# The last block's feed-forward in tiles of 128 rows, its elementwise steps on VectorE and ScalarE

## The chip, the cores and the metric

The kernel runs on one core of a Trainium2 chip. The metric is the device time of one execution in microseconds; the time of a kernel is the median of its runs. An execution under the profiler also leaves a trace, whose span runs from the first to the last instruction that it shows.

## The reference

One transformer layer in float32: attention with 16 heads of 16, a residual and a layer norm, then a gated feed-forward whose three products work on inputs and weights rounded to a 4-bit floating-point grid in blocks of 16, a residual and a layer norm. There are 4 sequences of 2048 rows of 256; the hidden width is 704.

```
def fp4_quant_dequant(x):                  # blocks of 16 along the last dim
    scale = max(max(|xb|) / 6, 1e-12)
    q = _GRID[searchsorted(_MID, |xb / scale|)] * sign(xb) * scale

x = layernorm(x + softmax(q @ k.T / 4) @ v @ Wo.T)
gate = fp4_linear(x, w_gate);  y = fp4_linear(x, w_up)
x = layernorm(x + fp4_linear(silu(gate) * y, w_down))
```

## The kernel before

The work is cut into blocks of 512 rows (QB), four to a sequence, 16 in all, and each block into four groups of four heads: 64 steps. A step has 16 periods, one per 128 rows of keys (NKT). In each period TensorE computes the row maxima's products for a step further ahead (pm, reduced by VectorE into mx), the products of keys and queries (pe, exponentiated by ScalarE into e), and adds the values into av. This is written out period by period in the program's main loop, and TensorE keeps that order.

Everything else is cut into pieces, generators that yield an estimate of what they cost, and the function period takes one piece (two before the first step) between the attention's parts of each period, from the deque queue, or from urgent for what the next step waits for. The elementwise steps that belong to a piece are put off by a few periods with later, so that no engine is asked for them too early. One such chain is a block's feed-forward: once its four groups are done, normalize has written the block's attention output, transposed, as two tiles oT (128 x 512), and chain(b, qb) is put into the queue. While the following block's attention runs, the pieces of feed_forward lie between its parts. The last block has no attention after it: after the main loop, a second loop runs periods until all deques are empty.

feed_forward first loads the block's 512 rows of x as x1 (four tiles of 128 rows). residual multiplies oT by woT (py), ScalarE copies the bank out (read), GpSimd adds it to x1, VectorE takes the moments, and layer_norm's other steps are GpSimd's. Quantization (fp4) works on two tiles of 128 rows at once: VectorE takes the blocks' maxima, scales, reciprocals and the rounding terms m; GpSimd multiplies by the reciprocal (line 157), adds and subtracts m (163, 164) and multiplies by the scale (165). TensorE transposes the result (ptq), ScalarE copies it to xqT. gated makes, for each tile of 128 rows and each half of the hidden width (352 columns), the products pg and pu; ScalarE copies them out as g and u and takes tanh of half of pg as a; three steps make h = (a * g + g) * u (lines 537, 538, 551). In the last block these three, and the second fp4's own engine steps, run on VectorE for tiles 1 and 3 and on GpSimd for 0 and 2; elsewhere always on GpSimd. h is quantized, transposed by TensorE (pth), copied to hT by ScalarE (turned, two tiles together), and down multiplies it by wdT: for each half of the 256 output columns six products of 128 columns (pz), which ScalarE copies out and GpSimd adds to x1. out_rows normalizes two tiles and stores them.

PSUM has three banks of the pool ps_x and, once the attention is over, alternately those of ps_m. The tiles e rotate over ten buffers. TensorE's queue holds its instructions in the order in which the code issues them; for the other engines the language's own scheduler places them, and may weave two independent sequences. Each engine then runs its queue in order, and engines wait for each other by semaphores. The stores and loads here are all issued by SP.

Of the kernel before, what the change touches and what calls it, by code (L numbers as in the profile page):

```python
# [33 lines left out]
I32 = mybir.dt.int32  # L34
# [17 lines left out]
LN_EPS = 1e-5  # L52
LEAD = 20
LAG = 2
LEAST = 300.0
PSUM = bass.MemoryType.PSUM
DRAM = bass.MemoryType.DRAM
# [16 lines left out]
def block_kernel(  # L74
# [41 lines left out]
    def later(periods, step, rest=0):  # L116

        state = {"done": None}
        due.append((clock["now"] + periods, step, state))
        return lambda: state["done"] is not None and clock["now"] >= state["done"] + rest  # L120
# [21 lines left out]
        nc.scalar.copy(t, bank)  # L142
        return t

    def fp4(pool, t, tag, gain=1.0, engine=None):
# [8 lines left out]
        engine = engine or nc.gpsimd  # L154
        engine.tensor_scalar(rs, rs, gain * TIES_DOWN, 1.0, ALU.mult, ALU.mult)
        xn = pool.tile([p, nb, FB], F32, tag="xn" + tag, name="xn", bufs=3 if tag else 2)
        engine.tensor_tensor(xn, t, rs.unsqueeze(2).to_broadcast([p, nb, FB]), ALU.mult)

        def rounded():
            m = pool.tile([p, nb, FB], F32, tag="m" + tag, name="m", bufs=1)  # L160
            nc.vector.tensor_single_scalar(m.bitcast(I32), xn.bitcast(I32), EXPONENT, ALU.bitwise_and)
            nc.vector.tensor_scalar(m, m, 1.0, ROUND, ALU.max, ALU.mult)  # L162
            engine.tensor_tensor(xn, xn, m, ALU.add)  # L163
            engine.tensor_tensor(xn, xn, m, ALU.subtract)  # L164
            engine.tensor_tensor(xn, xn, sc.unsqueeze(2).to_broadcast([p, nb, FB]), ALU.mult)  # L165

        return xn, later(1, rounded, 4 if tag == "" else 2)


    ident = const.tile([P, P], F32, tag="ident", name="ident")  # L170
# [252 lines left out]
    def exponentials(s, kt, i):  # L423
        kb, col = kt // QT, kt % QT * P
        pe = [psum("pe") for _ in range(2)]
        for j in range(2):
            rows = slice(R * j, R * j + R)
            matmul(pe[j], k_sb[s, i, kb][rows, col : col + P], q_sb[s, i][rows, :], start=True, stop=True)
        for j in range(2):
            e = p1.tile([P, QB], F32, tag="e", name="e", bufs=10)  # L430
            nc.scalar.activation(e, pe[j], AF.Exp, scale=SCALE)  # L431
            e_sb[s, kt, 2 * i + j] = e

# [83 lines left out]
                later(3, lambda tiles=tiles: xq.append(fp4(p2, tiles, "")))  # L517
            yield 900

    def gated(xqT, h, t, engine):  # L520
        for half in range(2):
            cols = slice(half * FH, (half + 1) * FH)
            pg = psum("pg")
            for kc in range(KC):
                matmul(
                    pg[:, :FH],
                    xqT[:, kc, t * P : (t + 1) * P],
                    wgT[:, kc, cols],
                    start=(kc == 0),
                    stop=(kc == KC - 1),  # L530
                )

# [3 lines left out]
            nc.scalar.activation(a, pg[:, :FH], AF.Tanh, scale=0.5)  # L536
            engine.tensor_mul(a, a, g)  # L537
            engine.tensor_add(a, a, g)  # L538
# [12 lines left out]
            engine.tensor_mul(h[:, cols], a, u)  # L551
            yield 1200

    def turned(hq, tiles, hT):
# [29 lines left out]

    def feed_forward(b, qb, between):
        rows = slice(qb * QB, (qb + 1) * QB)
        last = b == B - 1 and qb == NQB - 1
# [12 lines left out]
        for kc in range(KC):  # L600
            pt = psum("ptq")
            for t in range(QT):
                q = xq[t // 2][0].rearrange("p (t b) f -> p t (b f)", t=2)
                transpose(pt[:, t * P : (t + 1) * P], q[:, t % 2, kc * P : (kc + 1) * P], ident)
            nc.scalar.copy(xqT[:, kc, :], pt)
            yield 500
        hq = {}

        def gate(t):

            engine = nc.vector if last and t % 2 else nc.gpsimd
            h = p2.tile([P, FF], F32, tag="h", name="h")
            yield from gated(xqT, h, t, engine)
            blocks = h.rearrange("p (b f) -> p b f", f=FB)
            later(1, lambda: hq.update({t: fp4(p2, blocks, "h", gain=0.5, engine=engine)}))
# [23 lines left out]
        out_rows(2)  # L639


    queue, urgent = deque(), deque()
# [57 lines left out]
    for n in range(-LEAD, N + LAG):  # L700
        m = n + LEAD
        (sm, im), (s, kt), (sv, kv) = divmod(m, NKT), divmod(n, NKT), divmod(n - LAG, NKT)
        if m in (8, 10, 12, 14):
            if m == 8:
                load_q(1)
            load_k(1, m // 2 - 4)
        if n == 0:
            load_v(0)
        if kt == 3 and 0 <= n and s + 1 < len(steps):
            load_v(s + 1)  # L710
        if n > 0 and kt % QT == 0:
            ahead, kb = divmod(n - QT + 2 * NKT, NKT)
            if ahead < len(steps):
                b, qb, g = steps[ahead]
                c = str(g * HG // NC)
                if kb == 0:
                    assert (b, qb, "q" + c) in projected
                    load_q(ahead)
                assert (b, kb // QT, "k" + c) in projected
                load_k(ahead, kb // QT)  # L720

        for i in range(NP):
            if m < N:
# [12 lines left out]
        period(1 if n >= 0 else 2)  # L736
    banks["more"] = True
    while urgent or queue or due:
        period(1)

# [3 lines left out]
_INS = [  # L744
    "L0_attn_x",
# [29 lines left out]
```

## Time and profile before

| | |
|---|---|
| runs | 3693.88, 3696.45, 3697.93 us |
| median | 3696.45 us |
| profiled execution | 3695.37 us, its span 3693.6 us |
| granted TensorE clock, mean of the span | 0.982 of full speed |
| TensorE matmul busy | 3540.7 us (96%) |
| VectorE busy | 2805.0 us (76%) |
| ScalarE busy | 2694.0 us (73%) |
| GpSimd busy | 1293.4 us (35%) |
| last oT written by ScalarE | at 3604.2 us |
| end of the last arithmetic instruction | at 3690.4 us |

In the profile, PE is TensorE's matmul, PEld its weight loads, DVE is VectorE, ACT ScalarE, POOL GpSimd, SP the engine that issues the DMAs. A row of a group or of the order of time gives the line of the kernel, the engine, the operation, the tiles written and read with their shapes, and the time of one in microseconds or, where said, nanoseconds; in brackets stands how long the engine was idle before, and who ended that. Matmuls and transposes carry the line of a helper, so they are told apart by their tiles. The chain of waits follows the work that ended last back from its end, at each step to what released it.

### The profile page before, as it was taken

The numbers are of one execution on the slowest core, as the hardware profiler recorded it, in microseconds if no ns is written. First come the engines' busy times: TensorE is split into PE (matmuls) and PEld (weight loads), VectorE is DVE, ScalarE is ACT, GpSimd is POOL, SyncE is SP. The second block draws the span as 40 slices with busy tenths as digits, with TensorE's granted clock in tenths as the row PEclk, the third lists the DMA queues.
The fourth block names the chain that finished last, engine by engine and source line by source line (L and its number), as shares of the span: only waits on it lengthen the run. The fifth ranks groups of instructions, "written<-read, shape, count | busy, mean of one in ns | idle before, by whom it ended". The sixth has DMA issues, their size and how long they took to land.

```text
span 3693.6 us, 57860 instructions
## 1 busy us (share of the span) xinstructions
PE 3540.7 (96%) x21396; PEld 1602.0 (43%) x21396; DVE 2805.0 (76%) x3250; ACT 2694.0 (73%) x5452; POOL 1293.4 (35%) x1542
## 2 busy tenths in 40 slices
PE   5889999999999999999999999999999999999995
PEld 4433444444444444444444444444443434444343
DVE  3777777787787877878787787778778788878834
ACT  2667777777777777777777777777777777777772
POOL 0331432424243242423424243342424325241425
PEclk8899999999999999999999999999999999999997
DMA  6643333223232332323323232322322221222100
GB/s 217 188 137 117 93 91 105 81 85 115 68 114 84 94 94 85 109 70 109 95 78 106 85 97 88 97 89 74 113 75 63 75 79 57 75 68 86 47 7 6
DMA packets 197954, 334.18 MB, mean 90 GB/s; under 512 B 26024, under 2 KB 75560, under 8 KB 197672
## 3 DMA queue, kind: packets, MB, share of 16 engines
q1 hardware_dynamic: 196280, 329.16, 29.2%
q8 instruction: 171, 2.80, 0.3%
q10 hardware_dynamic: 1392, 1.31, 0.1%
q14 instruction: 111, 0.91, 0.1%
HBM read 242.81 MB, written 86.51 MB: 89 GB/s over the span
## 4 chain that ended last, share of the span: by engine, by line
PE 82%; DVE 11%; DMA 2%; POOL 2%; SPq 1%; issue 1%; ACT 1%; ACTq 0%; POOLq 0%; DVEq 0%
PE av L134 24%; PE pe L134 18%; PE pm L134 16%; DVE mx L397 8%; PE pz L134 5%; PE pg L134 5%; PE pu L134 5%; PE pq L134 3%; PE pth L137 1%; PE pv L134 1%; PE pa L137 1%; PE py L134 1%; PE pn L137 1%; DMA k<-kx 1%; DMA xb<-in_L_attn_x_dram 1%; DVE amax L149 1%
## 5 line engine op out<-in xcount | busy, mean ns | idle before, releaser
L397 DVE TENSOR_REDUCE mx<-pm 128x2 f32<-128x1024 f32 x2048 | 2407.9, 1217 | 706.8 <-PE pm L134 702.5
L431 ACT ACTIVATE e<-pe 128x512 f32<-128x512 f32 x4096 | 2217.9, 595 | 671.2 <-PE pe L134 666.0
L134 PE MATMUL av<-e,v 128*32 128x512 f32 x8192 | 1098.3, 608 | 0.0
L134 PE MATMUL pe<-q,k 64*128 64x512 f32 x4096 | 1037.2, 456 | 4.8 <-ACT e L431 4.4
L134 PEld LDWEIGHTS pe<-q,k 64*128 64x128 f32 x4096 | 476.4, 185 | 969.0 <-ACT e L431 855.7
L134 PE MATMUL pm<-k,q 62*128 62x512 f32 x4096 | 803.8, 448 | 60.0 <-DVE mx L397 53.0
L134 PEld LDWEIGHTS pm<-k,q 62*128 62x128 f32 x4096 | 347.0, 186 | 373.2 <-issue 178.6
L134 PEld LDWEIGHTS av<-e,v 128*32 128x32 f32 x8192 | 162.2, 108 | 332.2 <-issue 314.1
L537 POOL TENSOR_TENSOR a<-a,g 128x352 f32<-128x352 f32 x124 | 116.4, 939 | 499.5 <-ACT a L536 499.5
L582 POOL TENSOR_TENSOR x<-x,read 128x128 f32<-128x128 f32 x128 | 58.9, 460 | 493.6 <-ACT read L142 493.6
L134 PE MATMUL pz<-wdT,hT 128*128 128x128 f32 (+1 forms) x1536 | 230.0, 292 | 0.0
L163 POOL TENSOR_TENSOR xn<-xn,m 128x704 f32<-128x704 f32 (+2 forms) x104 | 159.5, 1534 | 157.7 <-DVE m L162 139.0
L134 PEld LDWEIGHTS pz<-wdT,hT 128*128 128x128 f32 (+1 forms) x1536 | 191.0, 191 | 45.5 <-ACT e L431 18.2
L551 POOL TENSOR_TENSOR h<-a,u 128x352 f32<-128x352 f32 x124 | 116.2, 937 | 226.7 <-ACT u L550 224.4
L134 PE MATMUL pg<-wgT,xqT 128*128 128x352 f32 x512 | 187.4, 489 | 0.0
L513 POOL TENSOR_TENSOR x<-x,read 128x256 f32<-128x256 f32 x64 | 46.7, 730 | 400.2 <-ACT read L142 399.9
L134 PE MATMUL pu<-wuT,xqT 128*128 128x352 f32 x512 | 186.1, 486 | 0.0
L164 POOL TENSOR_TENSOR xn<-xn,m 128x704 f32<-128x704 f32 (+2 forms) x104 | 159.8, 1536 | 5.6
L165 POOL TENSOR_TENSOR xn<-xn,sc 128x704 f32<-128x704 f32 (+2 forms) x104 | 131.5, 1264 | 7.8
L538 POOL TENSOR_TENSOR a<-a,g 128x352 f32<-128x352 f32 x124 | 118.8, 958 | 9.7
L134 PEld LDWEIGHTS pg<-wgT,xqT 128*128 128x128 f32 x512 | 88.3, 191 | 58.5 <-ACT e L431 19.1
L134 PEld LDWEIGHTS pu<-wuT,xqT 128*128 128x128 f32 x512 | 88.2, 191 | 58.7 <-ACT e L431 20.0
(95 smaller groups left out, 2283.1 us busy)
## 6 DMA issues: line engine op xcount, KB each, us to landing
k<-kx SPq DMA_DIRECT2D x1024, 128.0 KB
v<-vx SPq DMA_DIRECT2D x64, 768.0 KB
q<-qx SPq DMA_DIRECT2D x256, 124.0 KB
kx<-khi SPq DMA_DIRECT2D x64, 256.0 KB
qx<-qhi SPq DMA_DIRECT2D x64, 256.0 KB
xb<-in_L_attn_x_dram SPq DMA_DIRECT2D x27, 512.0 KB
vx<-vt SPq DMA_DIRECT2D x128, 96.0 KB
x<-in_L_attn_x_dram SPq DMA_DIRECT2D x16, 512.0 KB
```

The lines of the kernel that those rows point to most:

```text
L134: tc.keep_in_program_order(nc.tensor.matmul(*args, **kw))
L137: tc.keep_in_program_order(nc.tensor.transpose(*args))
L163: engine.tensor_tensor(xn, xn, m, ALU.add)
L164: engine.tensor_tensor(xn, xn, m, ALU.subtract)
L165: engine.tensor_tensor(xn, xn, sc.unsqueeze(2).to_broadcast([p, nb, FB]), ALU.mult)
L397: nc.vector.tensor_reduce(mx_sb[s][:, t, 2 * i : 2 * i + 2, kb], pm, AX.X, ALU.max)
L431: nc.scalar.activation(e, pe[j], AF.Exp, scale=SCALE)
L513: nc.gpsimd.tensor_add(x1[:, t, :], x1[:, t, :], read(py[:, :D]))
L537: engine.tensor_mul(a, a, g)
L538: engine.tensor_add(a, a, g)
L551: engine.tensor_mul(h[:, cols], a, u)
L582: nc.gpsimd.tensor_add(x1[:, t, cols], x1[:, t, cols], read(pz))
```

## The change

The block feed-forward of blocks 1 to 15 stays as it is, without the choice of engine that only the last block used. The last block is no longer put into the queue. When the deques are empty, a new function feed_forward_last writes out its work for single tiles of 128 rows, in an order given by hand in which the steps of up to four tiles alternate. Its x1 is loaded at the last step's first period.

All elementwise steps are on VectorE, except the two that make the reciprocal root of the variance, which stay on GpSimd (on one column), and those that ScalarE has: copies out of PSUM and tanh. py and pz are added to x1 by VectorE straight from PSUM, without the copy read. The layer norm subtracts the mean and multiplies in one VectorE instruction. (a + 1) * g is one instruction where it was two. fp4_at_once does the whole quantization of one tile on VectorE without delays. The products pg and pu of a half are issued together, and a, g and u live in buffers of e. down is one product of 256 columns per chunk, six of them per tile, each tile has its own three copies of hT, and each tile is stored alone (128 KB).

```diff
+    def fp4_at_once(pool, t, tag, gain=1.0):
+        step = nc.vector
...
+        step.tensor_reduce(amax, t, AX.X, ALU.max, apply_absolute_value=True)
...
+        step.tensor_scalar(sc, amax, gain / 6.0, 1e-12, ALU.mult, ALU.max)
...
+        step.reciprocal(rs, sc)
+        step.tensor_scalar(rs, rs, gain * TIES_DOWN, 1.0, ALU.mult, ALU.mult)
...
+        step.tensor_tensor(xn, t, rs.unsqueeze(2).to_broadcast([p, nb, FB]), ALU.mult)
...
+        step.tensor_single_scalar(m.bitcast(I32), xn.bitcast(I32), EXPONENT, ALU.bitwise_and)
+        step.tensor_scalar(m, m, 1.0, ROUND, ALU.max, ALU.mult)
+        step.tensor_tensor(xn, xn, m, ALU.add)
+        step.tensor_tensor(xn, xn, m, ALU.subtract)
+        step.tensor_tensor(xn, xn, sc.unsqueeze(2).to_broadcast([p, nb, FB]), ALU.mult)
+        return xn
...
+    def feed_forward_last(b, qb, x1):
...
+        def moments(t):
+            st = p2.tile([P, 6], F32, tag="st", name="st")
+            nc.vector.bn_stats(st, x1[:, t, :])
+            mv = p2.tile([P, 4, 2], F32, tag="mv", name="mv")
+            nc.vector.bn_aggr(mv[:, 0, :], st)
+            rstd = p2.tile([P, 2], F32, tag="rstd", name="rstd")
+            nc.gpsimd.tensor_scalar_add(rstd[:, :1], mv[:, 0, 1:2], LN_EPS)
+            nc.gpsimd.tensor_tensor(rstd[:, :1], rstd[:, :1], minus_half[:, :1], ALU.pow)
+            norms[t] = mv, rstd
+        def normed(t):
+            mv, rstd = norms.pop(t)
+            nc.vector.tensor_scalar(
+                x1[:, t, :], x1[:, t, :], mv[:, 0, 0:1], rstd[:, :1], ALU.subtract, ALU.mult
+            )
+        def attended(t):
...
+            nc.vector.tensor_add(x1[:, t, :], x1[:, t, :], py[:, :D])
+            moments(t)
+        def quantized(t):
+            normed(t)
+            xq[t] = fp4_at_once(p2, x1[:, t].rearrange("p (b f) -> p b f", f=FB), "")
+        def up(t):
...
+            nc.scalar.copy(xqT[:, :, t * P : (t + 1) * P], pt)
...
+                pg, pu = psum("pg"), psum("pu")
...
+                a, g, u = (wide(name)[:, :FH] for name in "agu")
+                nc.scalar.activation(a, pg[:, :FH], AF.Tanh, scale=0.5)
+                nc.scalar.copy(g, pg[:, :FH])
+                nc.scalar.copy(u, pu[:, :FH])
...
+        def hidden(t):
...
+                nc.vector.scalar_tensor_tensor(a, a, 1.0, g, ALU.add, ALU.mult)
+                nc.vector.tensor_mul(h[:, half * FH : (half + 1) * FH], a, u)
+            hq[t] = fp4_at_once(p2, h.rearrange("p (b f) -> p b f", f=FB), "h", gain=0.5)
+        def downward(t):
...
+                if c0 == 0:
+                    nc.scalar.copy(dst[:, :4, :].rearrange("p c n -> p (c n)"), pt)
+                    continue
+                for c in range(c0, NFC):
+                    w = min(P, FF - c * P)
+                    nc.scalar.copy(dst[:w, c, :], pt[:w, (c - c0) * P : (c - c0 + 1) * P])
+            pz = psum("pz")
+            for c in range(NFC):
+                w = min(P, FF - c * P)
+                matmul(pz[:, :D], dst[:w, c, :], wdT[:w, c, :], start=(c == 0), stop=(c == NFC - 1))
+            return pz
+        def added(t, pz):
+            nc.vector.tensor_add(x1[:, t, :], x1[:, t, :], pz[:, :D])
+            moments(t)
+        def stored(t):
+            normed(t)
+            at = qb * QB + t * P
+            nc.sync.dma_start(out[b, at : at + P, :], x1[:, t, :])
+        attended(0)
+        attended(1)
+        quantized(0)
+        up(0)
+        attended(2)
+        quantized(1)
+        up(1)
+        hidden(0)
+        attended(3)
+        quantized(2)
+        pz = downward(0)
+        up(2)
+        hidden(1)
+        added(0, pz)
+        quantized(3)
+        pz = downward(1)
+        up(3)
+        hidden(2)
+        stored(0)
+        added(1, pz)
+        pz = downward(2)
+        hidden(3)
+        stored(1)
+        added(2, pz)
+        pz = downward(3)
+        stored(2)
+        added(3, pz)
+        stored(3)
...
+        if n == N - NKT:
+            x1_last = load_last(*steps[-1][:2])
...
-            if sv % NG == NG - 1:
+            if sv % NG == NG - 1 and sv + 1 < len(steps):
                 queue.append(chain(*steps[sv][:2]))
...
+    feed_forward_last(*steps[-1][:2], x1_last)
```

More of the change, by code (lines that the diff above doesn't have):

```diff
@@ L54 @@
 LAG = 2
+E_BUFS = 10
 LEAST = 300.0
@@ L143, in read, with fp4 @@
         return t
-    def fp4(pool, t, tag, gain=1.0, engine=None):
+    def fp4(pool, t, tag, gain=1.0):
         p, nb, _ = t.shape
@@ L153, in fp4 @@
         nc.vector.reciprocal(rs, sc)
-        engine = engine or nc.gpsimd
-        engine.tensor_scalar(rs, rs, gain * TIES_DOWN, 1.0, ALU.mult, ALU.mult)
+        nc.gpsimd.tensor_scalar(rs, rs, gain * TIES_DOWN, 1.0, ALU.mult, ALU.mult)
         xn = pool.tile([p, nb, FB], F32, tag="xn" + tag, name="xn", bufs=3 if tag else 2)
-        engine.tensor_tensor(xn, t, rs.unsqueeze(2).to_broadcast([p, nb, FB]), ALU.mult)
+        nc.gpsimd.tensor_tensor(xn, t, rs.unsqueeze(2).to_broadcast([p, nb, FB]), ALU.mult)
         def rounded():
@@ L162, in rounded @@
             nc.vector.tensor_scalar(m, m, 1.0, ROUND, ALU.max, ALU.mult)
-            engine.tensor_tensor(xn, xn, m, ALU.add)
-            engine.tensor_tensor(xn, xn, m, ALU.subtract)
-            engine.tensor_tensor(xn, xn, sc.unsqueeze(2).to_broadcast([p, nb, FB]), ALU.mult)
+            nc.gpsimd.tensor_tensor(xn, xn, m, ALU.add)
+            nc.gpsimd.tensor_tensor(xn, xn, m, ALU.subtract)
+            nc.gpsimd.tensor_tensor(xn, xn, sc.unsqueeze(2).to_broadcast([p, nb, FB]), ALU.mult)
         return xn, later(1, rounded, 4 if tag == "" else 2)
+    def fp4_at_once(pool, t, tag, gain=1.0):
+        step = nc.vector
+        p, nb, _ = t.shape
+        amax = pool.tile([p, nb], F32, tag="amax" + tag, name="amax")
+        step.tensor_reduce(amax, t, AX.X, ALU.max, apply_absolute_value=True)
+        sc = pool.tile([p, nb], F32, tag="sc" + tag, name="sc")
+        step.tensor_scalar(sc, amax, gain / 6.0, 1e-12, ALU.mult, ALU.max)
+        rs = pool.tile([p, nb], F32, tag="rs" + tag, name="rs")
+        step.reciprocal(rs, sc)
+        step.tensor_scalar(rs, rs, gain * TIES_DOWN, 1.0, ALU.mult, ALU.mult)
+        xn = pool.tile([p, nb, FB], F32, tag="xn" + tag, name="xn", bufs=3 if tag else 2)
+        step.tensor_tensor(xn, t, rs.unsqueeze(2).to_broadcast([p, nb, FB]), ALU.mult)
+        m = pool.tile([p, nb, FB], F32, tag="m" + tag, name="m", bufs=1)
+        step.tensor_single_scalar(m.bitcast(I32), xn.bitcast(I32), EXPONENT, ALU.bitwise_and)
[4 more added lines that the diff above has]
+        return xn
     ident = const.tile([P, P], F32, tag="ident", name="ident")
@@ L429, in exponentials @@
         for j in range(2):
-            e = p1.tile([P, QB], F32, tag="e", name="e", bufs=10)
+            e = p1.tile([P, QB], F32, tag="e", name="e", bufs=E_BUFS)
             nc.scalar.activation(e, pe[j], AF.Exp, scale=SCALE)
@@ L518, in residual, with gated @@
             yield 900
-    def gated(xqT, h, t, engine):
+    def gated(xqT, h, t):
         for half in range(2):
@@ L536, in gated @@
             nc.scalar.activation(a, pg[:, :FH], AF.Tanh, scale=0.5)
-            engine.tensor_mul(a, a, g)
-            engine.tensor_add(a, a, g)
+            nc.gpsimd.tensor_mul(a, a, g)
+            nc.gpsimd.tensor_add(a, a, g)
             yield 1200
@@ L550, in gated @@
             nc.scalar.copy(u, pu[:, :FH])
-            engine.tensor_mul(h[:, cols], a, u)
+            nc.gpsimd.tensor_mul(h[:, cols], a, u)
             yield 1200
@@ L586, in feed_forward @@
         rows = slice(qb * QB, (qb + 1) * QB)
-        last = b == B - 1 and qb == NQB - 1
         x1 = p1.tile([P, QT, D], F32, tag="x1", name="x1", bufs=2)
@@ L609, in gate @@
         def gate(t):
-            engine = nc.vector if last and t % 2 else nc.gpsimd
             h = p2.tile([P, FF], F32, tag="h", name="h")
-            yield from gated(xqT, h, t, engine)
+            yield from gated(xqT, h, t)
             blocks = h.rearrange("p (b f) -> p b f", f=FB)
-            later(1, lambda: hq.update({t: fp4(p2, blocks, "h", gain=0.5, engine=engine)}))
+            later(1, lambda: hq.update({t: fp4(p2, blocks, "h", gain=0.5)}))
         def out_rows(t):
@@ L639, in feed_forward, with load_last, wide @@
         out_rows(2)
+    def load_last(b, qb):
+        x1 = p1.tile([P, QT, D], F32, tag="x1", name="x1", bufs=2)
+        nc.sync.dma_start(x1, x[b, qb * QB : (qb + 1) * QB, :].rearrange("(t p) d -> p t d", p=P))
+        return x1
+    def feed_forward_last(b, qb, x1):
+        heads = [oTs[(b * NQB + qb) * KC + c] for c in range(KC)]
+        xqT = p1.tile([P, KC, QB], F32, tag="xqT", name="xqT")
+        xq, gates, hq, hT, norms = {}, {}, {}, {}, {}
+        def wide(name):
+            return p1.tile([P, QB], F32, tag="e", name=name, bufs=E_BUFS)
+        def moments(t):
[13 more added lines that the diff above has]
+        def attended(t):
+            py = psum("py")
+            for c in range(KC):
+                matmul(
+                    py[:, :D], heads[c][:, t * P : (t + 1) * P], woT[:, c, :], start=(c == 0), stop=(c == KC - 1)
+                )
+            nc.vector.tensor_add(x1[:, t, :], x1[:, t, :], py[:, :D])
[4 more added lines that the diff above has]
+        def up(t):
+            pt = psum("ptq")[:, : KC * P].rearrange("p (k n) -> p k n", k=KC)
+            for kc in range(KC):
+                transpose(pt[:, kc, :], xq[t].rearrange("p b f -> p (b f)")[:, kc * P : (kc + 1) * P], ident)
+            nc.scalar.copy(xqT[:, :, t * P : (t + 1) * P], pt)
+            gates[t] = []
+            for half in range(2):
+                cols = slice(half * FH, (half + 1) * FH)
+                pg, pu = psum("pg"), psum("pu")
+                for bank, w in ((pg, wgT), (pu, wuT)):
+                    for kc in range(KC):
+                        matmul(
+                            bank[:, :FH],
+                            xqT[:, kc, t * P : (t + 1) * P],
+                            w[:, kc, cols],
+                            start=(kc == 0),
+                            stop=(kc == KC - 1),
+                        )
+                a, g, u = (wide(name)[:, :FH] for name in "agu")
+                nc.scalar.activation(a, pg[:, :FH], AF.Tanh, scale=0.5)
+                nc.scalar.copy(g, pg[:, :FH])
+                nc.scalar.copy(u, pu[:, :FH])
+                gates[t].append((a, g, u))
+        def hidden(t):
+            h = p2.tile([P, FF], F32, tag="h", name="h")
+            for half, (a, g, u) in enumerate(gates.pop(t)):
+                nc.vector.scalar_tensor_tensor(a, a, 1.0, g, ALU.add, ALU.mult)
+                nc.vector.tensor_mul(h[:, half * FH : (half + 1) * FH], a, u)
+            hq[t] = fp4_at_once(p2, h.rearrange("p (b f) -> p b f", f=FB), "h", gain=0.5)
+        def downward(t):
+            if t % 2 == 0:
+                hT[t // 2] = p2.tile([P, 2, NFC, P], F32, tag="hT", name="hT", bufs=1)
+            q, dst = hq[t].rearrange("p b f -> p (b f)"), hT[t // 2][:, t % 2]
+            for c0 in range(0, NFC, 4):
+                pt = psum("pth")
+                for c in range(c0, min(c0 + 4, NFC)):
+                    w = min(P, FF - c * P)
+                    transpose(pt[:w, (c - c0) * P : (c - c0 + 1) * P], q[:, c * P : c * P + w], ident)
+                if c0 == 0:
[6 more added lines that the diff above has]
+            for c in range(NFC):
+                w = min(P, FF - c * P)
+                matmul(pz[:, :D], dst[:w, c, :], wdT[:w, c, :], start=(c == 0), stop=(c == NFC - 1))
[35 more added lines that the diff above has]
+        stored(3)
```

## The prediction

> **What bounds the kernel now.** I read the granted clock first (0.982, one core, nothing disturbed), then the engines by stages, then the chain that ended last, then the order of time. By stages (columns: TensorE, weight loads, VectorE, ScalarE, GpSimd as "PE PEld DVE ACT POOL", busy us and instructions, then the granted TensorE clock, DMA share and GB/s):
>
> ```profile
> 3500.00:3600.70 100.70, 96.47 (x590) 41.80 (x590) 35.27 (x50) 76.29 (x154) 28.20 (x36) 1.00 0.05 14
> 3604.20:3627.70 23.50, 5.36 (x23) 4.02 (x23) 6.93 (x18) 2.07 (x5) 16.84 (x24) 0.66 0.00 0
> 3627.70:3648.40 20.70, 16.74 (x49) 10.18 (x48) 9.11 (x13) 8.19 (x19) 12.79 (x12) 0.89 0.01 2
> 3648.40:3666.50 18.10, 8.49 (x29) 5.93 (x30) 11.96 (x16) 3.90 (x9) 13.21 (x11) 0.62 0.00 0
> 3666.50:3679.00 12.50, 9.34 (x62) 8.07 (x61) 10.01 (x19) 2.69 (x7) 5.42 (x10) 0.91 0.00 1
> 3679.00:3690.40 11.40, 7.34 (x49) 6.30 (x47) 1.22 (x4) 1.70 (x6) 4.24 (x10) 0.95 0.07 24
> ```
>
> Until 3600.7 TensorE is 96% busy with attention. From 3604.2, when ScalarE has written the last block's last oT, nothing is left but that block's feed-forward, and no engine is full: it is a chain of waits. Its pieces (start, us, what):
>
> ```profile
> 3613.11 1.10 POOL x L497 x2
> 3614.59 1.07 POOL xn L157
> ...
> 3646.83 1.55 POOL xn L165
> ...
> 3679.05 7.30 PE pz L134 x48
> ...
> 3689.83 0.54 POOL x L497
> ```
>
> GpSimd carries most of it, first the quantization of x1 (xqT begins at 3626.3, 22 us after oT), then that of h; at the end 48 matmuls of 128 columns stand alone. The last arithmetic ends at 3690.4, and the last store takes the remaining 3.2 us of the 3693.6 span. So this stage is 3604.2 to 3690.4, **86.2 us**. The profiled run was 3695.4, 1.1 below the median of 3696.45; I put the difference of spans onto the median.
>
> **What does not move.** In the built program every engine's instructions, with their waits, stand in the same order up to the last block's first py; SP loads that block's x1 from the same place in its queue as before (issued at 3376.8, long landed). So everything up to 3604.2 is costed at nothing.
>
> **The new stage on VectorE.** It gets nearly all elementwise work: 128 instructions, 32 per tile of 128 rows. The rows that price them, with the contended one beside them:
>
> ```profile
> 3671.60 0.89 DVE L157 TENSOR_TENSOR xn<-h,rs 128x704 f32<-128x704 f32 x1
> 3667.45 0.53 DVE L551 TENSOR_TENSOR h<-a,u 128x352 f32<-128x352 f32 x1
> 3673.29 0.53 DVE L162 TENSOR_SCALAR m<-m 128x704 f32<-128x704 f32 x1
> 3663.66 1.68 POOL L164 TENSOR_TENSOR xn<-xn,m 128x704 f32<-128x704 f32 x1
> 3663.92 1.80 DVE L537 TENSOR_TENSOR a<-a,g 128x352 f32<-128x352 f32 x1 [2.15 <-ACT a L536]
> ```
>
> Two tensors in: 0.89 for 704 columns, 0.53 for 352, so 0.43 for 256 by the line through both. One tensor in: 0.53 for 704, 0.43 for 512 (rows of m), so 0.30 for 256. Maximum: 0.89 for 704, 0.69 for 512, so 0.42 for 256. Reciprocal: 0.43 for 44, 0.26 for 16. Moments 0.43 + 0.18; small steps 0.18. The normalization with its two operands of one column per row is at best 0.30, at worst the two-tensor 0.43 (eight of them: 1 us); an addition from PSUM I take as from SBUF, since oq's 128 columns from PSUM took 0.29, where the line gives 0.30. Per tile:
> - residual and moments: 0.43 + 0.43 + 0.18 = 1.04;
> - normalize and quantize 256 columns: 0.30 + 0.42 + 0.18 + 0.26 + 0.18 + 0.43 + 2 x 0.30 + 3 x 0.43 = 3.66;
> - gate (the fused add-and-multiply of two tensors, not in the trace, at the nearest row 0.53; from 0.3, if it ran like one tensor in, to 1.0, if it cost its two steps): 4 x 0.53 = 2.12, and quantizing h: 0.89 + 0.18 + 0.43 + 0.18 + 0.89 + 2 x 0.53 + 3 x 0.89 = 6.30;
> - down's addition, moments, last normalization: 1.34.
>
> 14.46 per tile, **57.8 us** for four. In the rows of before a VectorE step that depends on its predecessor starts 0.04 after its end, an independent one 0.09 before it; the order of the new program weaves two tiles, so about 90 of the 128 overlap and 8.4 us come off.
>
> **What VectorE waits for.** I stepped the new order with its waits through these durations. Each wait has a place:
> - py and residual before the first step 0.5; the variance goes to GpSimd (0.22 + 0.71) and back: 0.7, 0.7, 0.7, 0.6, 0.2, and 1.1 at the very end, 4.0 in all;
> - the first gate: ptq, its copy to xqT, two pg, tanh and copy, with nothing of another tile behind the waiting instruction that could go ahead of it: 0.8 with TensorE at full clock, 3.3 at half;
> - last, nothing covers pth, three copies, six pz of 256 columns: 2.4 at full clock, 4.5 at half. Full: a py of 256 columns steps 0.215, so six are 1.3 against 12 x 0.147 = 1.8 for two products of 128 columns;
> - the additions of pz in the middle stand in VectorE's queue ahead of the next tile's quantization, so a late pz holds that up: 0 at full clock, 0.9 and 0.7 at half.
>
> With dependent gaps of 0.8 this makes 57.7 us from oT to the last normalization at full clock throughout, and 64.0 with the clock falling in each pause over 3.4 us; 66 if TensorE never warmed.
>
> **The clock: row against rule.** Stages of before around two pauses of TensorE, granted clock third from the end:
>
> ```profile
> 3644.50:3648.40 3.90, 0.00 (x0) 0.00 (x0) 3.73 (x4) 1.26 (x3) 3.74 (x4) 1.00 0.00 0
> 3648.40:3649.10 0.70, 0.66 (x4) 0.42 (x4) 0.63 (x3) 0.00 (x0) 0.70 (x1) 1.00 0.00 0
> 3649.10:3658.60 9.50, 0.00 (x0) 0.00 (x0) 7.47 (x10) 0.59 (x1) 6.47 (x6) 0.52 0.00 0
> 3658.60:3662.70 4.10, 4.03 (x12) 3.05 (x13) 1.32 (x3) 1.22 (x3) 2.40 (x3) 0.50 0.00 0
> ```
>
> A pause of 3.9 us left the clock at 1.00, one of 9.5 brought it to 0.50 for 4.1 us of work (another of 3.2 us, to 3677.1, also ended at 0.50). The Trainium skill's page "TensorE: Matmul & The Clock Gate" (part 1, "What's actually happening") has half clock after at least one idle window of about 3.4 us, the windows running free. In the new order TensorE's pauses are 7.5 us before the first ptq, 7 before the first pth, and 4 to 5 before the later pth. If only the long ones cooled it, as the 3.9 us row alone would have it, the stage is 61.1; by the rule 64.0. I take 64.0, since the 3.2 us pause did cool.
>
> **What goes with GpSimd.** Its 16 remaining instructions are 3.7 us by their rows. That matters because of contention: 0.53 became 1.80 at 3663.92 while GpSimd ran. The page "SBUF — State Buffer" ("Who interferes with whom") says that a VectorE instruction with two SBUF inputs contends with a GpSimd one that reads SBUF. So I use uncontended prices: 57.8 of work; at 1.67 times for two-input steps (33 us of them) it would be 80.
>
> **Everything else hides.** ScalarE has 39 instructions, some 17 us at 0.27 to 0.59, and loses the eight read copies; its gate copies wait for buffers of e that VectorE frees, but those of tile 1 are free before needed, since VectorE itself needs the values later. Three of four stores leave early; the last has 128 KB where 256 KB took 3.2, so 2.8 to 3.2; I take 3.2.
>
> **Sum.** The same stepping, done for before from oT to xqT, where the engines still take turns, gives 21.6 against 22.1 measured, 2.5% short. 64.0 x 1.025 = 65.5 us; 3604.2 + 65.5 + 3.2 = 3672.9 of span, 20.7 below 3693.6. 3696.45 - 20.7 = **3675.7**.
>
> **Rivals.**
> - TensorE stays warm (12 in 100): for it, pg and pu come in bursts; against it, the 7 us pauses. 57.7 x 1.025 + 2.8 ends at 3666.1, time 3668.9.
> - VectorE's steps cost more in this order (15 in 100): inputs in PSUM, scalars from [128,1] operands, weaving that overlaps less. If the 8.4 us of overlap is lost, 64.0 becomes 72.4, time 3682.6. For it: 3671.31 plus 0.18 to 3671.60 left a gap of 0.11; against it, the overlaps seen among neighbours.
> - Slower than before (4 in 100): two-input steps at contended price throughout. 33 us of them must cost 20.7 more (a factor of 1.63) to break even; at the 1.80 / 0.53 = 3.4 of the row above the stage would be some 79 us longer, time over 3750. Against it: 3.7 us of GpSimd work, of which each can block one step.
> - The stage is not the end (3 in 100): another wait, such as the store of the block before, ends last, and the time stays near 3696. Nothing in the chain shows one.
> - The forecast: 66 in 100.
>
> **How the numbers follow.** The runs differ by 4 us in 3696 and I call 0.2%, 7.4 us, the least that a measurement can tell from no change. Below: full clock, the short store and the fused step at 0.3 (8 x 0.23 = 1.8 less), with the 2.5% left away on part: 3665. Above: lost overlap and 1 us of dearer normalizations, 3684. Between them lie forecast, warm and most of the dear case, over 8 in 10. Faster by over 0.2%: 66 + 12 + 15 = 93; within: 3; slower: 4.
>
> **What would show it.** After: first xqT about 9 us after oT (22 before); VectorE over 85% busy from there to the last pth; two-input steps at 0.43, 0.53 and 0.89; the clock near 0.5 to 0.7; GpSimd under 5 us; last normalization near 3670. Wrong, if the 256-column steps are over 0.5, if the fused step is near 1.0 (eight of them, 0.5 more each: 4 us), or if the head of VectorE's queue waits for a pz over 1 us at each tile.

## The result, and the profile after

| | before | changed |
|---|---|---|
| median | 3696.47 us (six runs, 3693.88 to 3698.36) | 3680.76 us (six runs, 3679.01 to 3681.75) |
| profiled execution, its span | 3695.37, 3693.6 | 3680.56, 3678.7 |
| last oT written | 3604.2 | 3607.6 |
| from there to the last normalization | 86.2 | 68.5 |
| from there to the end of the span | 3.2 | 2.6 |

The changed kernel takes 0.9958 of the time before (95% interval 0.9945 to 0.9971): 15.7 us less where 20.7 were forecast, inside the range of 3665 to 3684. The stages of the changed kernel, with the columns as in the prediction (PE, PEld, DVE, ACT, POOL, then clock, DMA share, GB/s), first as a whole and then in parts:

```profile
3607.60:3676.10 68.50, 46.45 (x158) 30.09 (x158) 49.88 (x128) 15.18 (x40) 8.52 (x16) 0.87 0.02 6
3607.60:3616.30 8.70, 1.58 (x7) 1.07 (x7) 6.48 (x24) 0.00 (x0) 1.61 (x4) 0.89 0.00 0
3616.30:3618.20 1.90, 1.44 (x4) 0.79 (x5) 1.71 (x5) 0.37 (x1) 0.00 (x0) 0.50 0.00 0
3618.20:3625.30 7.10, 7.10 (x22) 4.47 (x20) 1.99 (x4) 2.52 (x6) 0.00 (x0) 0.79 0.00 0
3625.30:3635.00 9.70, 5.98 (x22) 3.77 (x21) 9.05 (x24) 2.89 (x7) 0.77 (x2) 0.99 0.00 2
3646.90:3659.00 12.10, 9.30 (x36) 5.88 (x36) 11.12 (x28) 3.79 (x10) 1.02 (x2) 1.00 0.06 22
3666.80:3676.10 9.30, 6.46 (x18) 4.52 (x18) 1.86 (x5) 0.90 (x3) 1.39 (x4) 0.68 0.04 14
```

Before, no engine was full in this stage and GpSimd carried the chain; now VectorE is busy 9.05 of 9.7 us and 11.1 of 12.1 in the middle, where the chain runs along it. At two places it stands still while TensorE works: 3618.2 to 3625.3 (TensorE all 7.1 us, VectorE 2.0) and the last 9.3 us. VectorE's waits (us in total, times, longest):

```profile
DVE x L755 <- PE pz L135: 7.6, 4, 5.6
DVE x L685 <- POOL rstd L680: 4.4, 6, 1.0
DVE a L729 <- ACT g L722: 4.0, 2, 2.9
DVE x L695 <- PE py L135: 2.1, 1, 2.1
DVE h L730 <- ACT u L723: 1.2, 2, 0.9
```

(Of py's 2.1 us, 0.8 lie after the last oT.) VectorE's busy 49.9 us and 18.6 of pauses make up the 68.5. The pieces of the chain that answer to those before:

```profile
3616.29 0.70 PE ptq L138 x2
...
3617.44 2.71 PE pg L135 x4
...
3668.62 4.93 PE pz L135 x12
3673.58 0.43 DVE x L755
...
3675.67 0.41 DVE x L685
```

The first ptq comes 8.7 us after oT and its copy to xqT 9.4 us after it, where before that copy came 22.8 us after oT (the prediction's 22 is the ptq ahead of it). The end is again a string of pz products with nothing beside it: 12 rows in 4.93 us, where 48 took 7.30. In the order of time the same products stand at two speeds:

```profile
3617.44 2.71 PE L135 MATMUL pg<-wgT,xqT 128*128 128x352 f32 x4 [0.46 <-ACT xqT L706]
...
3621.77 1.35 PE L135 MATMUL pg<-wgT,xqT 128*128 128x352 f32 x4
...
3648.33 3.05 PE L135 MATMUL pz<-wdT,hT 128*128 128x256 f32 x12 [0.46 <-ACT hT L743]
...
3668.62 4.92 PE L135 MATMUL pz<-wdT,hT 128*128 128x256 f32 x12 [0.25 <-ACT hT L743]
```

Two things are to be read here. Every row counts twice what the code issues: up issues two pg per half, the row has x4; downward issues six pz, the row has x12. Each float32 product of the code thus stands in the trace as two matmuls; these are called passes below. And four passes of pg take 2.71 us after a pause of 7 us, 1.35 later; twelve of pz take 3.05 or 4.92.

VectorE's prices in the stage (busy us, mean ns):

```profile
L729 DVE SCALAR_TENSOR_TENSOR a<-a,g 128x352 f32<-128x352 f32 x8 | 4.1, 516 | 4.0 <-ACT g L722 4.0
L187 DVE TENSOR_TENSOR xn<-xn,sc 128x704 f32<-128x704 f32 x4 | 3.5, 886 | 0.0
L185 DVE TENSOR_TENSOR xn<-xn,m 128x256 f32<-128x256 f32 x4 | 1.7, 421 | 0.1
L184 DVE TENSOR_SCALAR m<-m 128x256 f32<-128x256 f32 x4 | 1.1, 288 | 0.0
L685 DVE TENSOR_SCALAR x<-x,mv,rstd 128x256 f32<-128x256 f32 x8 | 3.3, 410 | 4.4 <-POOL rstd L680 4.4
```

0.52, 0.89, 0.42 and 0.29 are the forecast prices (0.53, 0.89, 0.43, 0.30); only the normalization is near the upper of its two bounds (0.41 of 0.43).

### The profile page after: what moved, and what is told of

Read it like the earlier page. It is cut to its first block, busy times and chain, and to the rows that moved or that the text cites. A ratio compares the mean times of both kernels' runs of the same rounds, so it can differ in the third digit from the quotient of the medians.

```text
span 3678.7 us, 57761 instructions
## 1 busy us (share of the span) xinstructions
PE 3541.2 (96%) x21348; PEld 1597.4 (43%) x21348; DVE 2816.5 (77%) x3310; ACT 2690.0 (73%) x5446; POOL 1248.5 (34%) x1494
## 4 chain that ended last, share of the span: by engine, by line
PE 82%; DVE 12%; DMA 3%; POOL 1%; SPq 1%; ACT 1%; issue 0%; ACTq 0%; POOLq 0%; DVEq 0%
PE av L135 24%; PE pe L135 18%; PE pm L135 15%; DVE mx L418 8%; PE pz L135 6%; PE pg L135 5%; PE pu L135 5%; PE pq L135 3%; PE pv L135 2%; PE pth L138 1%; DMA q<-qx 1%; PE pa L138 1%; PE py L135 1%; PE pn L138 1%; DVE st L510 1%; DVE amax L150 1%
## 5 line engine op out<-in xcount | busy, mean ns | idle before, releaser
L558 POOL TENSOR_TENSOR a<-a,g 128x352 f32<-128x352 f32 x120 | 112.1, 934 | 494.6 <-ACT a L557 494.6
L135 PEld LDWEIGHTS pz<-wdT,hT 128*128 128x128 f32 x1488 | 188.6, 191 | 49.5 <-ACT e L452 18.2
L163 POOL TENSOR_TENSOR xn<-xn,m 128x704 f32<-128x704 f32 (+2 forms) x100 | 153.5, 1535 | 154.2 <-DVE m L162 135.7
L164 POOL TENSOR_TENSOR xn<-xn,m 128x704 f32<-128x704 f32 (+2 forms) x100 | 153.6, 1536 | 5.3
L559 POOL TENSOR_TENSOR a<-a,g 128x352 f32<-128x352 f32 x120 | 113.9, 949 | 9.4
```

Of the source, the lines that this page charges most:

```text
L135: tc.keep_in_program_order(nc.tensor.matmul(*args, **kw))
L163: nc.gpsimd.tensor_tensor(xn, xn, m, ALU.add)
L164: nc.gpsimd.tensor_tensor(xn, xn, m, ALU.subtract)
L558: nc.gpsimd.tensor_mul(a, a, g)
L559: nc.gpsimd.tensor_add(a, a, g)
```

## The experiments

The stage is always from the end of the last oT to the end of the last normalization in the run's profile, so it leaves out what scatters ahead of it. Two theories stood against each other in most of them: the gain is VectorE's prices in place of GpSimd's; or it is the small tiles and the woven order. And of the 5 us that were missing: TensorE's passes and clock, or VectorE, or something ahead of the stage.

### Is the stage all that changed?

The changed kernel unaltered, twice; the kernel before unaltered.

> The changed kernel once more, unaltered. Question: the changed kernel's last oT was written at 3607.6 us, the kernel before's at 3604.2, though every engine's order is the same up to there. If that is the scatter of single executions, this one falls anywhere from 3602 to 3609; if the change delays what lies ahead of the last block, it is again within 0.5 of 3607.6. In both cases the stage from the last oT to the last normalization stays at 68.5 within 0.7.

> The kernel before once more, unaltered. Its first profile had the last oT at 3604.2 us, that of the three kernels in the changed form at 3606.1 to 3608.4 (3607.6 twice for the changed kernel itself), that of the kernel before with VectorE alone at 3604.8. Theory A (scatter of single executions, set in the first 150 us where weights and x are loaded): this one lies anywhere from 3602 to 3609. Theory B (the changed form is late by some 3 us before its last block): 3604.2 to 3604.8 again. The stage from the last oT to the last normalization is 86.2 within 0.7 in both.

> The changed kernel timed beside the kernel before on the same chip, five rounds. The stage and the last store are together 18.3 us shorter than before by their profiles; the medians so far differ by 15.7. Theory A (what lies ahead of the last block is the same, and single executions scatter by some us): the medians differ by 16 to 20 here. Theory B (the changed form costs 2 to 3 us ahead of its last block): 15 to 16 again.

| run | last oT | stage | time |
|---|---|---|---|
| before, first profile | 3604.2 | 86.2 | 3695.4 |
| b0_again | 3605.7 | 86.15 | 3696.9 |
| changed, first profile | 3607.6 | 68.5 | 3680.6 |
| e0_again | 3607.6 | 69.15 | 3681.2 |
| e8_again_timed | 3606.8 | 71.75 | 3683.0 in the profiled run |

e8_again_timed: median 3679.91 (five runs) against 3697.67 (nine), 17.8 us, ratio 0.9953 (0.9940 to 0.9967). That is within theory A's 16 to 20. e0_again repeated the last oT of the first profile, 3607.6, which both of its cases allow; b0_again, at 3605.7, lies where theory A has it and outside theory B's 3604.2 to 3604.8. Time less last oT is 91.2 in both profiles of the kernel before, so its timed executions, 3691.9 to 3701.3 beside these experiments, had their last oT between 3600.7 and 3610.1; the changed form's nine profiles have it between 3604.1 and 3609.5. From the first oT written to the last, the three profiles in the form of before (e3_vector_alone, below, is the third) take 3349.3 to 3350.0 us and the nine of the changed form 3347.3 to 3351.4, both 3349.6 in the mean. The change shows no delay there; the rest of the scatter lies ahead of the first oT (254.1 to 259.3), where a delay of a microsecond or two can't be excluded by these runs.

The stage of the changed kernel is not 68.5 within 0.7 each time, though, as I had expected. In e8_again_timed VectorE's wait for pz is 10.9 us instead of 7.6:

```profile
DVE x L755 <- PE pz L135: 10.9, 4, 5.7
DVE x L685 <- POOL rstd L680: 4.4, 6, 1.0
```

and its clock by stages has two troughs between the first gate and the last pz, one down to 0.52, where the first profile had one, 0.86 from 3635.0 to 3646.9:

```profile
3634.00:3641.00 7.00, 6.66 (x18) 4.71 (x18) 4.16 (x13) 0.90 (x3) 1.30 (x2) 0.52 0.01 2
3641.00:3650.00 9.00, 7.46 (x30) 4.64 (x29) 8.69 (x24) 3.79 (x10) 1.66 (x2) 1.00 0.00 0
...
3658.00:3664.00 6.00, 3.73 (x13) 2.91 (x14) 5.76 (x11) 1.33 (x4) 0.00 (x0) 0.77 0.00 0
```

The first and the third pz of the same kernel ran at low clock here. Runs are therefore compared below where this pattern is alike.

### VectorE or the order

In e3_vector_alone the kernel before keeps its pairs, its order and its narrow products:

```diff
+        last = b == B - 1 and qb == NQB - 1
+        engine = nc.vector if last else nc.gpsimd
...
-                later(3, lambda tiles=tiles: xq.append(fp4(p2, tiles, "")))
+                later(3, lambda tiles=tiles: xq.append(fp4(p2, tiles, "", engine=engine)))
...
-            engine = nc.vector if last and t % 2 else nc.gpsimd
+            engine = nc.vector if last else nc.gpsimd
```

> The kernel before with its pairs of tiles, its order and its 128-column products, where in the last block gates and both quantizations are on VectorE for all four tiles (residual, variance, normalization and down's addition stay on GpSimd). Theory A (engine): with 52 us of VectorE work by the rows and little on GpSimd, 71 to 76 us from the last oT to the last normalization, against 86.2 before and 68.5 changed. Theory B (tiles and order): over 80.

The whole stage (columns as above) is 75.7 us, theory A, with GpSimd busy for 16.8 of it where it was 52.5 of 86.2:

```profile
3604.76:3680.43 75.67, 45.41 (x206) 33.54 (x206) 48.05 (x100) 18.57 (x46) 16.78 (x32) 0.82 0.01 4
```

In e2_gpsimd_quant the new form gives five steps of each quantization back to GpSimd:

```diff
-        step.tensor_scalar(rs, rs, gain * TIES_DOWN, 1.0, ALU.mult, ALU.mult)
+        nc.gpsimd.tensor_scalar(rs, rs, gain * TIES_DOWN, 1.0, ALU.mult, ALU.mult)
...
-        step.tensor_tensor(xn, t, rs.unsqueeze(2).to_broadcast([p, nb, FB]), ALU.mult)
+        nc.gpsimd.tensor_tensor(xn, t, rs.unsqueeze(2).to_broadcast([p, nb, FB]), ALU.mult)
...
```

(and so for the two with m and the one with sc.)

> The new tiles and the new order, but the five steps of each quantization that GpSimd had before (the factor on the reciprocal, the product with it, the two steps with m, the product with the scale) on GpSimd again. Theory A (what the change gains it gains by VectorE's prices, 0.88 against GpSimd's 1.5 to 1.8, and by having no second engine at the same SBUF): the stage is 80 to 90 us, most or all of the gain is gone, and VectorE's two-tensor steps of 352 columns, 0.52 now, are over 0.8 in the mean. Theory B (the gain is the tiles of 128 rows and the woven order): the stage stays under 74.

Stage 81.1: A again, but its sign for the second reason is missed. The groups:

```profile
L185 POOL TENSOR_TENSOR xn<-xn,m 128x704 f32<-128x704 f32 x4 | 6.9, 1736 | 4.8 <-DVE m L184 4.8
...
L685 DVE TENSOR_SCALAR x<-x,mv,rstd 128x256 f32<-128x256 f32 x8 | 5.8, 727 | 14.5 <-POOL rstd L680 14.5
L730 DVE TENSOR_TENSOR h<-a,u 128x352 f32<-128x352 f32 x8 | 5.7, 712 | 1.9 <-ACT u L723 1.4
...
L729 DVE SCALAR_TENSOR_TENSOR a<-a,g 128x352 f32<-128x352 f32 x8 | 4.9, 612 | 5.7 <-ACT g L722 5.7
...
L183 DVE TENSOR_SCALAR m<-xn 128x256 int32<-128x256 int32 x4 | 3.8, 949 | 5.6 <-POOL xn L181 3.6 <-POOL xn L186 2.0
```

VectorE's two-tensor steps of 352 columns rose from 0.52 to 0.71 and 0.61, not over 0.8. But contention shows in other steps: those with one tensor in rose more, the normalization from 0.41 to 0.73 and m of 256 columns from 0.29 to 0.95. One m took 1.75 us (from 3648.05) while GpSimd's step beside it ran from 3647.97 for 1.68. By the rows, the steps that stay on VectorE in both runs take some 10 us longer in all. To this come GpSimd's price (1.74 against 0.88) and new waits:

```profile
DVE x L685 <- POOL rstd L680: 14.5, 8, 3.8
DVE m L183 <- POOL xn L181: 7.2, 5, 2.4
```

The variance's root, 0.8 us of work, stands in GpSimd's queue behind quantization, and VectorE's normalization waits for it 14.5 us instead of 4.4. How the 12.6 us between this run and the first profile (81.1 to 68.5) divide among price, contention and waits is not shown. So with the old form the engine alone is worth 10.5 us (86.2 to 75.7), and the new form with most of quantization on GpSimd 5.1 (86.2 to 81.1); together 14.4 to 17.7. The larger part of the gain is the engine's. The 4 to 7 us from e3_vector_alone to the changed kernel hold, among others, the small tiles, the woven order, the residual and down's addition straight from PSUM, the shorter normalization and the wide product; only the last was taken apart.

### The wide product

```diff
-            for c in range(NFC):
-                w = min(P, FF - c * P)
-                matmul(pz[:, :D], dst[:w, c, :], wdT[:w, c, :], start=(c == 0), stop=(c == NFC - 1))
+            for n in range(KC):
+                cols = slice(n * P, (n + 1) * P)
+                for c in range(NFC):
+                    w = min(P, FF - c * P)
+                    matmul(pz[:, cols], dst[:w, c, :], wdT[:w, c, cols], start=(c == 0), stop=(c == NFC - 1))
```

> down again as two products of 128 columns per tile, all else as changed. Theory A (a product of float32 is two passes through TensorE, 256 columns 0.256 us a pass warm, 128 columns 0.147, so 12 passes become 24): each tile's down grows from 3.07 to 3.5 at full clock and from 4.9 to 6 or 7 where the clock is low; only the last one and the late one in the middle are waited for, so the stage goes from 68.5 to 69.5 to 72. Theory B (the wide product does nothing, or the last wait is something else's): 68.5 within 0.5.

Stage 71.3, theory A. The last down of that run:

```profile
3668.42 6.38 PE L135 MATMUL pz<-wdT,hT 128*128 128x128 f32 x24 [0.46 <-ACT hT L743]
```

24 passes, as two per product say. VectorE waited 10.1 us for pz; in e0_again, where the third pz was at full speed as here, 7.9. The wide product is worth some 2 us (71.3 against 69.15, one execution each).

### TensorE's clock

e4_warm puts products that nobody reads into the pauses, in three places; e6_warm_last only into the last; e7_warm_four into four.

```diff
+        def warm(n):
+            spare = ps_av.tile([P, QB], F32, tag="av", name="spare")
+            for _ in range(n):
+                matmul(spare[:, :FH], ident, wgT[:, 0, :FH], start=True, stop=True)
...
         quantized(0)
+        warm(10)
         up(0)
...
+        warm(5)
         pz = downward(0)
...
+        warm(5)
         pz = downward(3)
```

> The changed kernel with products of ident and wgT into a bank that nobody reads, placed in TensorE's queue where it would pause: ten (some 5.9 us at full clock) before the first ptq, five (3 us) before the first pth and five before the last pth. Nothing else is altered. Theory A (the waits for the first gate and for the last pz are long because TensorE's clock has fallen in the pause): the granted clock over the stage is over 0.95, the last 12 passes take 3.1 instead of 4.9, the first gate comes 2 us earlier, and the stage is 62 to 64 instead of 68.5; the time is 4 to 6 us lower. Theory B (the passes are slow there for another reason, such as copies that arrive one by one): the stage stays at 68.5 within 0.7, or grows by up to 2 if the extra products are in the way.

Stage 63.8, in theory A's range. Median 3673.81 against 3699.28, ratio 0.9927 (0.9913 to 0.9940). Its order of time, with the row of the extra products first:

```profile
3662.84 3.23 PE L135 MATMUL spare<-wgT,ident 128*128 128x352 f32 x10
...
3667.61 3.05 PE L135 MATMUL pz<-wdT,hT 128*128 128x256 f32 x12 [0.46 <-ACT hT L743]
...
3670.69 0.42 DVE L760 TENSOR_TENSOR x<-x,pz 128x256 f32<-128x256 f32 x1 [3.31 <-PE pz L135]
```

The twelve last passes take 3.05 instead of 4.92, and VectorE waits for them 3.31 instead of 5.64. The first gate's waits fell from 5.2 to 3.0 (2.94 to 1.43 at the first step). Beside the kernel before it is 25.5 us faster, where the changed kernel was 15.7 and 17.8: more than the 4 to 6 expected. Over the stage the clock was 0.97, as theory A has it, but not in every part, see the last row but one:

```profile
3647.00:3659.00 12.00, 9.21 (x36) 5.78 (x35) 10.92 (x25) 3.79 (x10) 1.03 (x2) 0.96 0.06 22
3659.00:3667.00 8.00, 7.79 (x28) 5.07 (x26) 5.47 (x12) 0.03 (x1) 1.38 (x2) 0.85 0.00 0
3667.00:3673.00 6.00, 3.20 (x14) 2.11 (x12) 1.63 (x5) 0.87 (x3) 0.78 (x2) 1.00 0.06 22
```

It fell after a pause of only 1.8 us, before the third pth. The same pause stands in the first profile, where the clock did not fall; its rows:

```profile
3659.03 0.87 PE L138 MATMUL pth<-ident,xn 128*128 128x128 f32 x6 [1.81 <-DVE xn L187]
3660.41 3.05 PE L135 MATMUL pz<-wdT,hT 128*128 128x256 f32 x12 [0.51 <-ACT hT L743]
```

and those of e4_warm:

```profile
3657.05 0.87 PE L138 MATMUL pth<-ident,xn 128*128 128x128 f32 x6 [1.81 <-DVE xn L187]
3658.43 4.47 PE L135 MATMUL pz<-wdT,hT 128*128 128x256 f32 x12 [0.51 <-ACT hT L743]
```

Of the six profiles with this pause of 1.81 us, the third pz ran at full speed in three (the first, e0_again, e1_two_products) and slowly in three (e4_warm, e6_warm_last, e8_again_timed). e7_warm_four fills it too (warm(3) ahead of downward(2)).

> The kernel with extra products in three places, and three more (1.8 us) before the third pth, where TensorE paused for 1.8 us and its clock fell for the third pz, for which VectorE then waited 1.64. Theory A (every pause counts, short ones too[...]): the granted clock is over 0.97 in every part of the stage, VectorE's wait for the third pz is under 0.3, the stage is 62 to 63 against 63.8 and the time some 1 us lower than that kernel's. Theory B (a pause of 1.8 us doesn't matter): the stage is 63.8 within 0.5.

```profile
3647.00:3659.00 12.00, 10.99 (x44) 6.94 (x43) 10.86 (x25) 3.79 (x10) 1.02 (x2) 1.00 0.06 22
3659.00:3667.00 8.00, 7.54 (x32) 5.05 (x31) 5.47 (x10) 0.90 (x3) 0.77 (x2) 1.00 0.06 18
3667.00:3671.00 4.00, 1.50 (x7) 0.71 (x5) 1.40 (x4) 0.00 (x0) 0.78 (x2) 1.00 0.00 0
```

Stage 62.1, clock 1.00 in every part, the wait for the third pz gone: theory A's numbers. Since the pause left unfilled was harmless in three of six profiles, this single one can't show that filling it was the cause. Median 3672.33 against 3697.67, ratio 0.9934 (0.9921 to 0.9946), and 7.6 us under the changed kernel timed beside it. The fourth place did not show in the times: the two warmed kernels are 25.5 and 25.3 us faster than the kernel before timed beside each.

> As the kernel with extra products in three places, but only the five before the last pth. Theory A (clock): only the last wait shrinks, pth from 1.5 to 0.9 and the 12 passes from 4.9 to 3.1, so the stage is 65.8 to 66.5. Theory B: 68.5 within 0.7.

Stage 68.7, theory B's number, for a reason that neither theory has. Its last wait fell to 3.31 as A says, but its first and third pz ran at low clock, as in e8_again_timed:

```profile
3631.50:3639.00 7.50, 6.79 (x20) 4.36 (x20) 4.51 (x15) 1.28 (x4) 1.30 (x2) 0.61 0.01 2
3656.00:3660.00 4.00, 2.95 (x11) 2.33 (x12) 3.79 (x8) 0.91 (x3) 0.00 (x0) 0.72 0.00 0
```

with waits of 2.99 and 1.82 for them (3.15 and 1.90 there). Both lie ahead of the inserted products in TensorE's queue, so those can't have caused it. Against e8_again_timed, which has the same pattern, the stage is 3.0 shorter, 2.36 of it in the last wait. The expectation failed because I took the changed kernel's stage as one number.

### The way to GpSimd and back

```diff
-            nc.gpsimd.tensor_scalar_add(rstd[:, :1], mv[:, 0, 1:2], LN_EPS)
-            nc.gpsimd.tensor_tensor(rstd[:, :1], rstd[:, :1], minus_half[:, :1], ALU.pow)
+            nc.vector.tensor_scalar(rstd[:, :1], mv[:, 0, 1:2], LN_EPS, 1.0, ALU.add, ALU.mult)
+            nc.vector.reciprocal(rstd[:, :1], rstd[:, :1])
```

> The changed kernel with the variance's reciprocal root left out: a plain reciprocal on VectorE stands in its place, so GpSimd has nothing to do in the stage and VectorE never waits for it; the normalization is therefore not the reference's. Theory A (each way to GpSimd and back costs VectorE what the records show, 4.4 us in six waits): with eight pairs of small steps more on VectorE (2 us, half of them hidden among neighbours) the stage is 65 to 67. Theory B (other waits take their place, because TensorE's results come no earlier): 68 to 69.

Stage 65.1, theory A: 3.4 us below the first profile of the changed kernel, 4.1 below e0_again. VectorE's waits:

```profile
DVE x L755 <- PE pz L135: 6.3, 1, 6.3
DVE a L729 <- ACT g L722: 4.5, 3, 2.9
...
DVE h L730 <- ACT u L723: 1.8, 2, 1.5
```

Against the first profile the six waits (4.4) are gone and VectorE is busy 0.95 longer (50.83 against 49.88). The waits for pz shrank by 1.3 and those for the first gates grew by 1.1, which nearly cancels. So the six waits are worth about what the records show.

## Why the prediction was right, and where its sizes were off

**What does not move.** Held from the first oT to the last (3349.6 us in the mean in both forms). That the first six runs show 15.7 us and the profiles' stage and store 18.3 is within the interval of the ratio, 10.7 to 20.3 us.

**VectorE's work.** 57.8 us by rows less 8.4 of overlap, 49.4; measured 57.45 by rows, 7.6 of it overlapped, 49.9 busy. Every bounded price came in at the value taken or, for the normalization, near its upper bound.

**What VectorE waits for: the step that was mis-sized.** The places are those named; the sizes were too small wherever a product of TensorE is in them. I priced a product as one pass ("six are 1.3 against 12 x 0.147 = 1.8"); it is two, so six of 256 columns are 3.05 at full clock against 24 x 0.147 = 3.5. The row that I quoted had 48 pz where the code issues 24. By places, at low clock in the changed kernel, and at full clock in e7_warm_four:

| wait | forecast, low clock | measured | forecast, full clock | e7_warm_four |
|---|---|---|---|---|
| py | 0.5 | 0.8 | 0.5 | 0.8 |
| variance and back | 4.0 | 4.4 | 4.0 | 4.7 |
| first gate | 3.3 | 5.2 | 0.8 | 3.0 |
| pz in the middle | 1.6 | 2.0 (5.3 in e8_again_timed) | 0 | 0.2 |
| last pz | 4.5 | 5.6 | 2.4 | 3.0 |

At low clock this is 4.1 us more, which carries 64.0 to 68.1; the 2.5% that I added for what stepping leaves out covered part of it, so 65.5 was 3.0 short of 68.5. At full clock, where no trough can be blamed, it is 4.0 more, and carries 57.7 to 61.7; 62.1 was measured. The last store took 2.6, not 3.2. The forecast change of stage and store was 20.7; 18.3 was measured.

**The clock, row against rule.** That the first gate and the last pz ran at low clock is as forecast, but in part by luck. Except for the first (7.1), the pauses were shorter than I had stepped them: 3.3 us where I had 7 before the first pth, then 0.6, 1.8 and 3.4 where I had 4 to 5. The rule of the Trainium skill's page "TensorE: Matmul & The Clock Gate" (part 1, "What's actually happening"), half clock after an idle window of about 3.4 us, was a better guide than the row with 3.9 us at full clock. But with these pauses it would hardly have cooled TensorE after the first one, while slow passes followed the pauses of 3.3 and 3.4 in every profile of the changed kernel, and that of 1.8 in one of three. With the pauses filled the stage lost 6.4 us (68.5 to 62.1).

**GpSimd's contention.** That taking the work off GpSimd pays is shown (12.6 us for the five steps, 81.1 to 68.5). That freeing the shared SBUF access is part of it shows in VectorE's rows of e2_gpsimd_quant. The prediction counted on two-tensor steps alone there (0.52 to 0.61 and 0.71); the steps with one tensor in rose more (0.41 to 0.73, 0.29 to 0.95). How large that part is stays open. GpSimd's remaining work was counted at half: 16 instructions at 0.22 and 0.71 are 7.4 us and not 3.7, and 8.5 were measured.

**The rivals.** TensorE staying warm did not happen by itself; made to happen, it gave a median of 3672.3, where 3668.9 had been worked out for it. VectorE's steps were not dearer, and 7.6 of the 8.4 us of overlap were kept; the 3682.6 worked out for that rival leaves away the 2.5% that the others have, with it it is 3684.4. The slower case needed 1.63 times the two-tensor price; in e2_gpsimd_quant, with GpSimd busy for 43.9 of 81.1 us, it was 1.2 to 1.4. The stage was the end. Of the signs, VectorE was busy 82% from the first xqT to the last pth where over 85% was forecast, and GpSimd 8.5 us where under 5 was; none of the signs of being wrong appeared (a pz was late by over 1 us at two of the four tiles).

## What to carry to other kernels

At the end of a kernel, where engines take turns, sum the work of the engine that is to carry the chain, and then each wait at which nothing else stands behind it in its queue; here the first sum was good to 1%, and the error lay in the second. Count TensorE's work in the instructions of the trace, not in the products of the code. Where a stage leaves TensorE idle for a few microseconds before a product that others wait for, a few products that nobody reads, placed in its queue ahead of that product, are cheap: here they shortened a stage of 68.5 us to 62.1.

## What the runs showed of the hardware that was not expected

- The same kernel's stage took 68.5, 69.15 and 71.75 us in three executions, although its order is fixed; the difference lies in which pz fell into a stretch of low clock (granted 0.52 from 3634 to 3641 in the longest, the first and third pz slow; in the others only the first pz was slow in part, and the last in all three).
- A pause of TensorE of 1.8 us was followed by slow passes in three of six profiles (12 passes in 4.5 to 4.7 us instead of 3.05), and by full clock in the other three; one of 3.9 us, before the change, by a stretch at 1.00.
- In e2_gpsimd_quant, while GpSimd worked, VectorE's steps with one tensor in were held up more than those with two: m of 256 columns took 0.95 us in the mean instead of 0.29, a two-tensor step of 352 columns 0.61 and 0.71 instead of 0.52.
- A normalization of 256 columns with two operands of one column per row takes 0.41 us, as much as a two-tensor step, where one with constants takes 0.29.
